# First loads in another order, paired layer 0 runs, and attention's gathers tied to the fourth maximum of a step

## The chip, the core and the metric

The kernel runs on one core of a Trainium2 chip. The core has five engines that work beside each other: TensorE (PE, matmuls and transposes into PSUM), VectorE (DVE), ScalarE (ACT), GpSimd (POOL) and SyncE (SP, which here only starts transfers). The metric is the device time of one execution in microseconds (us), given as the median over several runs.

## What is computed

Four residual layers follow each other on an input of 64 sequences with 64 tokens of 512 features, all in fp32. Each layer is conditional: token arrays pick which weights a sequence uses.

```python
x = x + (einsum('bsi,bio->bso', x, W0[id0]) + b0[id0][:, None])          # layer 0, 16 experts
x = x + (x @ W1 + ((x @ A[id1].T) @ Bm[id1].T) * scalings[id1])          # layer 1, 8 adapters
x = x + attention(x, Wq, Wk, Wv, Wo, k_blocks, v_blocks, tables, kv_lens) # layer 2
x = x + (einsum('bct,bcd->bdt', x, W3[id3]) + side[id3][:, :, None])     # layer 3, 8 subjects

# attention: 8 heads, 4 kv heads, head size 64; q and k are RMS-normed and rotated,
# new k and v are written into a paged cache (blocks of 16) at kv_lens ...,
# each token sees the 256 positions up to its own; softmax over scores * 256 ** -0.5
```

## The kernel before, in words

The 4096 tokens are cut into NT = 32 tiles of 128 tokens, two sequences each. The order of instructions on every engine is the order in which the program is written, since the framework's own scheduler is turned off; waits between engines are semaphores that the framework puts in. An instruction that waits holds up all that is behind it on its engine. SP's transfers also wait for their semaphore lane: eight lanes are used in turn.

**First part.** It makes layers 0 and 1 and the q, k and v of layer 2. `load_x` and `load_w0` bring a tile's input, transposed, and the two 512x512 expert matrices of its two sequences (1 MiB each, `wp` has four buffers, `load_next(i)` asks two tiles ahead). `layer0` multiplies, ACT copies the product to `s0` (L252), POOL adds the bias to x in `add_bias` (L260), PE turns `s0` and DVE adds it in `turn0` (L273, L274): that is x after layer 0, transposed. `layer1` (L612 to L649) takes the tiles in groups, `GROUPS = [1, 1, 2] + [4] * 7`: adapter products `pxa` (L620), masked on DVE into `xa` (L625), the dense products `p1` (L635), and a last product with `xa` (L643), for which PE waits on DVE. `turn_x2` turns a result, `product` makes q or kv (L140), and `turned` (L116 to L135) norms and rotates, on ACT, DVE and POOL. `keep_kv` stores k and v in `kvd`, a copy in DRAM that also gets the old cache rows (`copies`, gathered by POOL and written by SP, L155 and L161). The main loop (L709 to L738) goes over groups: behind layer 1 of group g comes, for each tile of group g + 1, layer 0, `load_next`, `other`, `turn0`, and for each tile of group g `turn_x2`, the q of an earlier tile, and `keep_kv`.

Two things run in pieces beside this on DVE. `rotation(o)` (L365) makes the sines and cosines of eight tiles; `rotation(0)` is made whole behind layer 1 of tile 0. `windows()` (L427) works out the gather indices; `other(i)` takes two of its pieces per tile. `scalars` (L399) prepares the norm gains, `epst`, `eye2` and the first adapter scale.

At the start the token arrays come in by five transfers: `tok1` on SP for register loads, and on ACT's queue `idcol`, `toki` (all tokens in every partition) and later `kvi`, twice; ACT's queue also carries `invf`, `gain` and `tabi`, and half of tile 0's W0, in four chunks.

**Attention.** In step s of the loop at L976, `scores(s)` makes eight score products of 128x320 (L842); DVE adds the mask and finds a maximum for each (L850), ACT takes exponentials with sums (L854). Then PE does `attend(s - 1)` (L889, result copied by DVE at L907), in even steps from 4 on two products of layer 3 (`last`, L929), `project(s - 2)` (L917, added by DVE at L921), `keys(s + 1)` (transposes L823 and L829, copied by ACT to `kT`) and `turn(s)`: 20 transposes of the normalised weights (L875, L879), copied to `pT` by DVE and ACT in turn (L876, L880). DVE normalises at L866, between L907 and L921. All of these but the projection share seven PSUM banks in turn (`ring`), so the third score product waits for the bank of the first pT copy of the step before.

`load_kv(i)` is five gathers on POOL (L769) of 128 rows each, 256 KB, into one of four `kv` buffers. Step s calls it for tile s + 2 at its top; only in steps 0 and 1 a small POOL copy (`after_keys`, L774) holds it until the keys of s are copied. The buffer of tile s + 2 is that of tile s - 2, which `attend(s - 2)` leaves free in step s - 1, so POOL, which has little else, starts the gathers there. Behind them on POOL is `add_one(s - 2)` (L815), which adds the identity to a W3 tile that SP loaded (`load_pair`).

## Time and profile before

| what | value |
|---|---|
| median of 9 runs | 976.68 us (973.21 to 981.08) |
| the profiled execution | 982.19 us, span 980.2 us |
| mean granted TensorE clock | 0.995 |
| PE busy | 933.1 us (95%) |
| DVE, ACT, POOL busy | 608.5, 412.8, 403.3 us |
| DMA | 260.97 MB, 266 GB/s over the span |

In the timeline a row has its start, its length, the engine, the line, the operation, the tile it writes and what it reads, and in brackets how long the engine stood idle before it and what ended that. A row can stand for several like it (x4), its length is then that of all together. In the chain of waits a row is a piece of the chain that ended last. In a table of windows a row has a stretch of time, its length, the busy time and the count of instructions of PE, weight loads, DVE, ACT and POOL, the granted clock, the busy share of DMA and its GB/s.

### The profile page before, as it was taken

To read this page: it belongs to the slowest core of one execution; us is meant where nothing else is said; L and a number is where in the kernel's file an instruction comes from. 1 tells how busy PE (TensorE), PEld (TensorE's weight loads), DVE (VectorE), ACT (ScalarE), POOL (GpSimd) and SP (SyncE) were. 2 spreads that over 40 slices of the span, in tenths; PEclk is the share of its full clock that TensorE was granted. 3 is DMA by queue.
4 is the path that set the end of the run, shared out by engine and by line. 5 is a ranking of instruction groups with operands and counts; after the bars stand their busy time and mean duration, and the time that the engine had idled before them with its cause. 6 is when DMAs were issued, how large, how long until landed. Compare 5 with 4: busy or idle time off the path is not lost.

```text
span 980.2 us, 17784 instructions
## 1 busy us (share of the span) xinstructions
PE 933.1 (95%) x5397; PEld 506.4 (52%) x5397; DVE 608.5 (62%) x1736; ACT 412.8 (42%) x1084; POOL 403.3 (41%) x599
## 2 busy tenths in 40 slices
PE   5999999999999999999999879999999999999998
PEld 1343443444444444444344546766666666666665
DVE  3756898878572363542226858666677666676673
ACT  0212134222341323422223655656666666666663
POOL 3343365554453444444425433444433333344400
PEclk9999999999999999999999989999999999999999
DMA  7988999999999999999954674666565556666521
GB/s 237 348 310 306 371 371 325 387 374 331 391 337 376 391 328 384 364 365 386 342 215 136 219 248 143 210 216 202 179 200 181 186 186 199 195 203 200 185 78 44
DMA packets 133344, 260.97 MB, mean 266 GB/s; under 512 B 32737, under 2 KB 41570, under 8 KB 133250
## 3 DMA queue, kind: packets, MB, share of 16 engines
q1 hardware_dynamic: 108562, 178.61, 50.8%
q0 software_dynamic: 23280, 79.84, 24.5%
q10 hardware_dynamic: 1408, 1.39, 0.5%
q8 instruction: 43, 0.70, 0.3%
q14 instruction: 51, 0.42, 0.1%
HBM read 190.29 MB, written 69.50 MB: 265 GB/s over the span
## 4 chain that ended last, share of the span: by engine, by line
PE 51%; DMA 4%; SPq 2%; DVE 2%; issue 1%; ACT 1%; POOL 0%; ACTq 0%; DVEq 0%; POOLq 0%; another core or an unknown queue 0%
PE py L917 12%; PE po L889 8%; PE ps L842 8%; PE ppt L875 5%; PE pk L140 3%; PE p L635 3%; PE pq L140 2%; PE pkt L823 2%; PE ppt L879 2%; PE p L249 1%; DMA kvd<-st 1%; PE pkt L829 1%; PE pz L929 1%; DMA w<-in_W 1%; DMA st<-in_kvc,cidx 1%
## 5 line engine op out<-in xcount | busy, mean ns | idle before, releaser
L769 POOL DMA_INDIRECT kv<-kvd,idxn x128 | 126.1, 985 | 216.2 <-PE po L889 159.2
L854 ACT ACTIVATE pr<-pr,mx 128x320 f32<-128x320 f32 x256 | 140.1, 550 | 6.3 <-DVE mx L850 3.0
L249 PE MATMUL p<-w,xt 128*64 128x512 f32 x512 | 123.0, 603 | 13.0 <-DMA w<-in_W 12.5
L917 PE MATMUL py<-wo,oT 128*128 128x512 f32 (+1 forms) x264 | 118.3, 592 | 1.7 <-DVE qn L128 1.7
L140 PE MATMUL pk<-wkv,x 128*128 128x512 f32 x256 | 117.1, 602 | 2.7 <-ACT x L656 2.7
L155 POOL DMA_INDIRECT st<-in_kvc,cidx x68 | 67.8, 997 | 113.3 <-DMA kvd<-st 97.3
L635 PE MATMUL p<-w,x 128*128 128x512 f32 x256 | 112.5, 596 | 0.0
L140 PE MATMUL pq<-wq,x 128*128 128x512 f32 x248 | 111.3, 593 | 0.0
L850 DVE CUSTOM_DVE_ANT_0 pr<-ps,mb 128x320 f32<-128x320 f32 x256 | 107.7, 486 | 5.8 <-PE ps L842 2.4
L842 PE MATMUL ps<-kT,qT 64*128 64x320 f32 x512 | 87.4, 460 | 13.4 <-DVE pT L876 8.2
L876 DVE COPY pT<-ppt 128x512 f32<-128x512 f32 x64 | 41.8, 687 | 77.4 <-PE ppt L875 36.0
L866 DVE TENSOR_SCALAR pr<-pr,sm 128x320 f32<-128x320 f32 x256 | 85.4, 395 | 2.3
L889 PE MATMUL po<-pT,kv 128*64 128x128 f32 (+1 forms) x1536 | 84.8, 282 | 1.6 <-issue 1.6
L274 DVE TENSOR_TENSOR x<-pt,x 128x512 f32<-128x512 f32 x32 | 22.0, 688 | 98.2 <-PE pt L273 54.9
L889 PEld LDWEIGHTS po<-pT,kv 128*64 128x64 f32 (+1 forms) x1536 | 70.9, 138 | 22.4 <-DVE mx L850 14.0
L917 PEld LDWEIGHTS py<-wo,oT 128*128 128x128 f32 x264 | 47.5, 189 | 61.6 <-issue 58.4
L249 PEld LDWEIGHTS p<-w,xt 128*64 128x64 f32 x512 | 35.6, 137 | 83.9 <-issue 70.7
L635 PEld LDWEIGHTS p<-w,x 128*128 128x128 f32 x256 | 47.8, 190 | 58.2 <-issue 56.5
L135 POOL TENSOR_TENSOR qr<-qn,sq 128x512 f32<-128x512 f32 x25 | 31.7, 1267 | 106.2 <-DVE qn L134 106.2
L140 PEld LDWEIGHTS pk<-wkv,x 128*128 128x128 f32 x256 | 47.0, 193 | 52.2 <-issue 48.3
L133 DVE TENSOR_TENSOR sq<-qn,sg 128x256 f32<-128x256 f32 (+1 forms) x128 | 40.1, 355 | 49.7 <-POOL sg L110 47.7
L140 PEld LDWEIGHTS pq<-wq,x 128*128 128x128 f32 x248 | 44.9, 190 | 46.2 <-issue 46.2
(191 smaller groups left out, 1322.9 us busy)
## 6 DMA issues: line engine op xcount, KB each, us to landing
w<-in_W SPq DMA_DIRECT2D x62, 1024.0 KB
kvd<-st SPq DMA_DIRECT2D x68, 512.0 KB
xt<-in_xT SPq DMA_DIRECT2D x32, 256.0 KB
x2d<-x2n SPq DMA_DIRECT2D x32, 256.0 KB
kvd<-kvn SPq DMA_DIRECT2D x32, 256.0 KB
qTd<-qTs SPq DMA_DIRECT2D x32, 256.0 KB
qT<-qTd SPq DMA_DIRECT2D x32, 256.0 KB
x2r<-x2d SPq DMA_DIRECT2D x32, 256.0 KB
```

What stands on the lines that cost most here:

```text
L140: TE.matmul(ps, x2s[i][:, c, :], w[:, c, :], start=c == 0, stop=c == KC - 1)
L155: P.indirect_dma_start(out=st, out_offset=None, in_=a["kvc"].rearrange("(n r) d -> n (r d)", r=2), in_offset=bass.IndirectOffsetOnAxis(ap= ...
L249: TE.matmul(p0[hs, :], xs[i][:, c, hs], w0s[i][h][:, c, :], start=c == 0, stop=c == KC - 1)
L635: TE.matmul(p1[i], x1s[i][:, c, :], w1[:, c, :], start=c == 0, stop=False)
L769: P.indirect_dma_start(out=kv[:, n, :], out_offset=None, in_=kvd, in_offset=bass.IndirectOffsetOnAxis(ap=at, axis=0),)
L842: TE.matmul(ps[g2][:, :NPOS], qT[rows, gp, b2].rearrange("p h t -> p (h t)"), kT[rows, gp, b2 * NPOS : (b2 + 1) * NPOS], start=True, stop= ...
L850: V.tensor_tensor_reduce(out=p, in0=ps[g2][:, :NPOS], in1=mb[:, b2, :], scale=-1.0, scalar=3.0e38, op0=ALU.add, op1=ALU.min, accum_out=mx[ ...
L854: S.activation(p, p, AF.Exp, bias=mx[:, g, b2 : b2 + 1], scale=-1.0, accum_out=sm[:, g, b2 : b2 + 1],)
L866: V.tensor_scalar(p, p, sm[:, g, b2 : b2 + 1], None, ALU.mult)
L875: TE.transpose(pt[:, n * 128 : (n + 1) * 128], pr[:, g, at : at + 128], ident)
L889: TE.matmul(po[b2][g2 * 64 : (g2 + 1) * 64, gp * 128 : (gp + 1) * 128], kv[rows, n, (G + g) * HD : (G + g + 1) * HD], pT[rows, c, m * 128 ...
L917: TE.matmul(py[:, fs], oT[:, c].rearrange("p b t -> p (b t)"), wo[:, c, fs], start=c == 0, stop=c == KC - 1,)
```

## The change

**The start.** `idcol`, `toki` and `kvi` are no longer loaded: DVE makes `tok1` a row of floats and PE spreads it by small matmuls into a PSUM bank, from which they are read or cast. `invf`, `gain` and `tabi` go to SP, behind `wkv`. The chunks of tile 0's W0 are issued in turn on SP and ACT with both row numbers read first. The bias is turned ahead of the last chunk's products, and `turn0(0)` is done in two halves. `scalars` keeps the gains alone and moves, with `rotation(0)`, behind `turn0(1)`.

**Layer 0 in pairs.** Where the next group is twice as large, the first tile of a pair keeps its `s0` (two buffers now) and is turned behind the second one's layer 0. `other` takes none of the windows' pieces at tile 1 and four at tile 2.

**Attention.** `keys(0)` moves ahead of the last q product of the passage. In every step the gathers of tile s + 2 come behind `scores(s)`, and a POOL copy of the fourth maximum of that step stands in front of them.

```diff
         nc.sync.dma_start(tok1.rearrange("p k b -> p (k b)"), a["toks"])
-        idcol = su.tile([B, 1], I32, name="idcol")
-        nc.scalar.dma_start(idcol, a["toks"][:, 0:B].rearrange("o b -> b o"))
-        toki = su.tile([128, 4, B], I32, name="toki")
-        nc.scalar.dma_start(toki.rearrange("p k b -> p (k b)"), a["toks"].partition_broadcast(128))
-        invf = su.tile([128, HALF], F32, name="invf")
-        nc.scalar.dma_start(invf, a["invf"].partition_broadcast(128))
-        nc.scalar.dma_start(
-            gain.rearrange("p k h f -> p (k h f)"), a["gains"].partition_broadcast(128)
-        )
         make_identity(nc, ident)
...
         P.iota(pidx, pattern=[[0, 1]], base=0, channel_multiplier=1)
+        one = su.tile([1, 128], F32, name="one")
+        V.memset(one, 1.0)
+        tokf = su.tile([1, 4, B], F32, name="tokf")
+        V.tensor_copy(tokf, tok1)
+        ptok = bank("ptok")
+        TE.matmul(ptok[:B, 4 * B : 4 * B + 1], tokf[:, 0, :], one[:, :1], start=True, stop=True)
+        for h in range(2):
+            TE.matmul(
+                ptok[h * B : (h + 1) * B, 4 * B + 1 : 4 * B + 2], tokf[:, 3, :], one[:, :1], start=True, stop=True
+            )
+        TE.matmul(ptok[:, : 4 * B], one, tokf.rearrange("p k b -> p (k b)"), start=True, stop=True)
+        toki = ptok[:, : 4 * B].rearrange("p (k b) -> p k b", k=4)
+        idcol = su.tile([B, 1], I32, name="idcol")
+        V.tensor_copy(idcol, ptok[:B, 4 * B : 4 * B + 1])
+        kvi = su.tile([128, 1], I32, name="kvi")
+        V.tensor_copy(kvi, ptok[:, 4 * B + 1 : 4 * B + 2])
         brow = su.tile([B, D], F32, name="brow", tag="valp")
...
-            w0s[i] = []
-            for b, queue in zip((2 * i, 2 * i + 1), queues):
-                w = wp.tile([128, KC, D], F32, name="w")
-                r = queue.value_load(tok1[0:1, 0, b : b + 1], min_val=0, max_val=E - 1)
-                for n in range(parts):
-                    cs = slice(n * KC // parts, (n + 1) * KC // parts)
-                    queue.dma_start(
-                        w[:, cs], a["W0"][bass.ds(r, 1)].rearrange("a (c p) o -> p (a c) o", p=128)[:, cs]
+            w0s[i] = [wp.tile([128, KC, D], F32, name="w") for _ in range(2)]
+            def row(h):
+                b = 2 * i + h
+                return queues[h].value_load(tok1[0:1, 0, b : b + 1], min_val=0, max_val=E - 1)
+            first = [row(h) for h in range(2)] if parts > 1 else []
+            for n in range(parts):
+                cs = slice(n * KC // parts, (n + 1) * KC // parts)
+                for h in range(2):
+                    r = first[h] if first else row(h)
+                    queues[h].dma_start(
+                        w0s[i][h][:, cs],
+                        a["W0"][bass.ds(r, 1)].rearrange("a (c p) o -> p (a c) o", p=128)[:, cs],
                     )
-                w0s[i].append(w)
...
             for c in range(KC):
+                if c == KC - 1 and not bias:
+                    turn_bias()
                 for h in range(2):
...
             w0s.pop(i)
-            s0 = s0s[i] = wk.tile([128, D], F32, name="s0")
+            s0 = s0s[i] = wk.tile([128, D], F32, name="s0", bufs=2)
             S.copy(s0, p0)
...
-        def turn0(i):
+        def turn0(i, parts=1):
...
             pt = bank("pt")
-            for c in range(KC):
-                TE.transpose(pt[:, c * 128 : (c + 1) * 128], s0[:, c * 128 : (c + 1) * 128], ident)
-            V.tensor_tensor(x1, pt.rearrange("p (c t) -> p c t", c=KC), x1, ALU.add)
+            for n in range(parts):
+                lo, hi = n * KC // parts, (n + 1) * KC // parts
+                for c in range(lo, hi):
+                    TE.transpose(pt[:, c * 128 : (c + 1) * 128], s0[:, c * 128 : (c + 1) * 128], ident)
+                V.tensor_tensor(
+                    x1[:, lo:hi], pt[:, lo * 128 : hi * 128].rearrange("p (c t) -> p c t", t=128), x1[:, lo:hi], ALU.add
+                )
...
         load_weight(wkv, "wkvT")
-        kvi = su.tile([128, 1], I32, name="kvi")
+        invf = su.tile([128, HALF], F32, name="invf")
+        nc.sync.dma_start(invf, a["invf"].partition_broadcast(128))
+        nc.sync.dma_start(gain.rearrange("p k h f -> p (k h f)"), a["gains"].partition_broadcast(128))
         tabi = su.tile([128, NBLK], I32, name="tabi")
         for h in range(2):
-            hs = slice(h * B, (h + 1) * B)
-            nc.scalar.dma_start(kvi[hs], a["toks"][:, 3 * B :].rearrange("o b -> b o"))
-            nc.scalar.dma_start(tabi[hs], a["tab"])
+            nc.sync.dma_start(tabi[h * B : (h + 1) * B], a["tab"])
...
         adf = su.tile([128, 8, 8], F32, name="adf")
-        V.tensor_copy(adf.rearrange("p o q -> p (o q)"), toki[:, 1, :])
-        V.tensor_tensor(adf, adf, bc(mine[:, None, :], [128, 8, 8]), ALU.mult)
+        V.tensor_tensor(
+            adf, toki[:, 1, :].rearrange("p (o q) -> p o q", q=8), bc(mine[:, None, :], [128, 8, 8]), ALU.mult
+        )
         ado = su.tile([128, 8], F32, name="ado")
...
             V.tensor_copy(gsw[:, :, 1, :], gain[:, :, 0, :])
-            V.memset(epst, EPS)
-            V.tensor_tensor(eye2, ident[:, :64], ident[:, 64:], ALU.add)
-            scale_b(0)
+        V.memset(epst, EPS)
+        V.tensor_tensor(eye2, ident[:, :64], ident[:, 64:], ALU.add)
+        scale_b(0)
...
         bg, old, turns, asked, made = windows(), copies(kvd[:OLD], op, 3), {}, [], []
+        held = []
...
-        scalars()
         biasT = su.tile([128, KC, B], F32, name="biasT")
+        def turn_bias():
+            pb = bank("pb")
+            for c in range(KC):
+                TE.transpose(pb[:, c * B : (c + 1) * B], brow[:, c * 128 : (c + 1) * 128], ident[:B, :B])
+            S.copy(biasT.rearrange("p c b -> p (c b)"), pb[:, : KC * B])
         layer0(0, False)
-        pb = bank("pb")
-        for c in range(KC):
-            TE.transpose(pb[:, c * B : (c + 1) * B], brow[:, c * 128 : (c + 1) * 128], ident[:B, :B])
-        S.copy(biasT.rearrange("p c b -> p (c b)"), pb[:, : KC * B])
         add_bias(0)
-        turn0(0)
+        turn0(0, 2)
         load_next(0)
...
-            next(bg, None)
-            next(bg, None)
+            for _ in range(0 if i == 1 else 4 if i == 2 else 2):
+                next(bg, None)
...
             layer1(tiles[g])
-            if g == 0:
-                run(rotation(0))
-            elif g == 1:
+            if g == 1:
                 far()
...
                     load_b(i0 // 4 + 1)
-                if i is not None:
-                    turn_x2(i)
-                q = asked.pop() if asked and i is not None else None
+                if i is None:
+                    held.append(i0)
+                    continue
+                turn_x2(i)
+                if held:
+                    turn0(held.pop())
+                q = asked.pop() if asked else None
                 if q is not None:
...
                 turn0(i0)
+                if g == 0:
+                    scalars()
+                    run(rotation(0))
                 if q is not None:
...
                     made.append(q)
-                if i is not None:
-                    keep_kv(i, product(i, wkv, "pk"), P)
-                    if i < NT - LATE:
-                        asked.append(i)
-                    if len(made) > 1:
-                        turn_q(made.pop(0))
+                keep_kv(i, product(i, wkv, "pk"), P)
+                if i < NT - LATE:
+                    asked.append(i)
+                if len(made) > 1:
+                    turn_q(made.pop(0))
         layer1(tiles[-1])
...
-    kvs, kTs, mbs, prs, pTs, oTs, qTs, pairs, x3s = {}, {}, {}, {}, {}, {}, {}, {}, {}
+    kvs, kTs, mbs, prs, mxs, pTs, oTs, qTs, pairs, x3s = {}, {}, {}, {}, {}, {}, {}, {}, {}, {}
...
-    def after_keys(i):
+    def after_scores(i):
         seen = bp.tile([1, 1], F32, name="seen")
-        P.tensor_copy(seen, kTs[i][0:1, 0, 0:1])
+        P.tensor_copy(seen, mxs[i][0][0:1, 1, 1:2])
...
         pr = bp.tile([128, G, 2 * NPOS], F32, name="pr")
-        mx = bp.tile([128, G, 2], F32, name="mx")
+        mxs[i] = [bp.tile([128, 2, 2], F32, name=f"mx{gp}") for gp in range(2)]
         sm = bp.tile([128, G, 2], F32, name="sm")
...
                         out=p, in0=ps[g2][:, :NPOS], in1=mb[:, b2, :], scale=-1.0, scalar=3.0e38,
-                        op0=ALU.add, op1=ALU.min, accum_out=mx[:, g, b2 : b2 + 1],
+                        op0=ALU.add, op1=ALU.min, accum_out=mxs[i][gp][:, g2, b2 : b2 + 1],
                     )
                     S.activation(
-                        p, p, AF.Exp, bias=mx[:, g, b2 : b2 + 1], scale=-1.0, accum_out=sm[:, g, b2 : b2 + 1],
+                        p, p, AF.Exp, bias=mxs[i][gp][:, g2, b2 : b2 + 1], scale=-1.0, accum_out=sm[:, g, b2 : b2 + 1],
                     )
...
     for i in range(NT - LATE + 1, NT - 1):
+        if i == NT - 2:
+            keys(0)
         pq = product(i, wq, "pq")
...
         next(parts[i])
-    keys(0)
     load_q(1)
...
         if s + 2 < NT:
-            if s < 2:
-                after_keys(s)
-            load_kv(s + 2)
             load_mask(s + 2)
...
         scores(s)
+        if s + 2 < NT:
+            after_scores(s)
+            load_kv(s + 2)
         if s >= 2:
...
         if s:
```

## The prediction

> **What bounds the kernel now.** I read the page first, then the chain of waits, the timeline of the first 60 us, of 540 to 610 us and of two late attention steps, and last the windows around 580 us. The page says that TensorE is the bound nearly everywhere:
>
> ```profile
> span 980.2 us, 17784 instructions
> PE 933.1 (95%) x5397; PEld 506.4 (52%) x5397; DVE 608.5 (62%) x1736; ACT 412.8 (42%) x1084; POOL 403.3 (41%) x599
> PEclk9999999999999999999999989999999999999999
> ```
>
> So only 47 us are without a matmul, and a gain must come out of these, or out of time in which PE is counted as busy but slow. They lie in three places. The first is the start: layer 0 of tile 0 ends at 16.6 us, and later PE waits for the next weights.
>
> ```profile
> 3.90 4.44 ACTq L232 DMA_DIRECT2D w<-in_W  x4
> 18.70 1.57 SPq L232 DMA_DIRECT2D w<-in_W  x2
> 19.82 1.09 PE L620 MATMUL pxa<-x,ao 128*32 128x128 f32 x8 [1.90 <-DVE x L274]
> 28.03 3.65 PE L249 MATMUL p<-w,xt 128*64 128x512 f32 x14 [1.44 <-DMA w<-in_W]
> ```
>
> The second is the passage into attention: a 2.9 us stall, then 6.8 us at half clock (0.50 in the third row).
>
> ```profile
> 576.77 2.01 PE L842 MATMUL ps<-kT,qT 64*128 64x320 f32 x10 [2.92 <-ACT pT L876]
> 575.00:580.00 5.00, 2.63 (x11) 1.52 (x12) 2.46 (x7) 3.82 (x7) 0.25 (x1) 0.84 0.73 234
> 580.00:585.00 5.00, 5.00 (x46) 3.93 (x48) 2.20 (x12) 4.99 (x16) 0.00 (x0) 0.50 0.24 65
> ```
>
> The third is every attention step. Here is the same spot twice, in a step with gathers and in one of the last steps, which have none:
>
> ```profile
> 849.73 1.91 PE L875 MATMUL ppt<-ident,pr 128*128 128x128 f32 x16
> 849.80 0.95 POOL L769 DMA_INDIRECT kv<-kvd,idxh  x1 [0.30 <-issue]
> 851.92 1.29 DVE L876 COPY pT<-ppt 128x512 f32<-128x512 f32 x2 [2.39 <-PE ppt L875]
> ...
> 951.19 1.91 PE L875 MATMUL ppt<-ident,pr 128*128 128x128 f32 x16
> 951.83 0.69 DVE L876 COPY pT<-ppt 128x512 f32<-128x512 f32 x1 [0.84 <-PE ppt L875]
> ```
>
> Without gathers the first pT copy starts 0.64 us behind the first transpose; with them 2.19 us, and ACT's starts beside it (852.04). In nearly all the steps with gathers it starts 1.1 to 1.3 us after the fifth gather's issue ends (850.75 here). The trace's semaphore events say how: PE's signals come on time until about 4.5 us after the first gather, then stop but for a stray one, and from 7.2 us on drain 0.06 us apart. The chain shows what the late copies cost, since scores need their banks:
>
> ```profile
> 915.23 0.74 PE ps L842 x4
> 916.00 0.70 DVE pT L876
> 916.74 1.95 PE ps L842 x12
> ...
> 928.95 2.58 PE ps L842 x16
> ...
> 940.93 2.35 PE ps L842 x16
> ...
> 953.54 2.35 PE ps L842 x16
> ```
>
> From scores to scores, an even step (with L929's two products, 0.86 us) takes 13.72 us with gathers and 12.61 without; an odd one 11.98, and 12.61 - 0.86 = 11.75 without.
>
> **The start, cost by cost.** Out go six DMAs of token data and constants in front of ACT's half of W0, and lane waits behind them (SP's third and fourth chunk are issued at 5.68 and 7.81, as toki and gain land). In come three small DVE operations (0.15 to 0.2 us each) and a handful of tiny matmuls (0.3 us each at most); all of it, under 2 us, fits between the tokens' landing at 3.4 and the first W0 landing at 8.7, so it costs nothing; without that cover, 2 us. SP gains four issues (invf, gain, twice tabi, 0.4 to 0.6 each, 2 us) behind wkv; queued behind them are tile 2's loads, landed at 41.3 for a use at 42.3, with SP some 6 us earlier: nothing.
>
> DMA moved 356 GB/s at 10 to 15 us, 210 at 15 to 20. With x and W0 of tile 0 (2.36 MB) first, from 3.5 us, they are in by 10.1, with landing 11.3, against 15.5. The bias is turned ahead of the last chunk's matmuls, its 1.47 us on POOL leave the path, and turn0 in halves gives up 0.3 more: pxa at 15.5 instead of 19.82. The bias gather can eat 1 us of this (it took 7.8 us to land). W0 of tile 1 (2.1 MB, behind w1 and the gathers) lands near 21.6, so layer 0 of tile 1 ends at 25.3 instead of 31.6.
>
> But DVE takes it back. rotation(0), 21.37 to 28.93 = 7.6 us, and scalars, 1.1, used to run beside layer 1 of tile 0; now they stand behind turn0(1), at 27.1. Then the kv chain (ACT square to xa, 36.68 to 40.78 = 4.1, plus 0.4 for the cosine): xa at 40.3, before 40.8. PE has only pk, pxa and p1 to do and waits some 5 us. Two window steps (28.85 to 33.86, 5.0) move to tile 2, where DVE runs without a gap: mask to 44.0, four steps 10.2, two more 5.5, two turn0 1.4, so x1 of tile 3 at 61.1 and pxa at 61.2, before 59.36: 1.8 late. The pairs take away ACT's copy of s0 from PE's path: 0.77 each at 46.7 (inside that wait), 72.9 and 90.8, so 1.5 won. Sum: 0.3 lost. Bounds: 4 won, if DVE gets its gain rows earlier and PE keeps its lead; 3 lost, if POOL slows DVE. I take 0.3 lost, as the DVE rows add up to it.
>
> **The passage.** keys(0) goes ahead of the last q product: its 1.1 us and the 0.98 wait leave PE's path, but DVE starts the first maxima at 552.77 either way; 0.8 is left. The gathers for tile 2 move from 551.6 to 555.1, so their quiet end (7.2 later, 562.3) now delays step 0's pT by 2.5: scores(1) end at 565.0, 1.2 late. Those for tile 3 start at 566 (before 560.4), tile 4's at 577 (before 568.8), out of the stretch in which DMA was 0.92 to 1.05 busy. Then scores(2) run to 576 instead of 580.8, po at full clock, py waits 1.8 for DVE's qn as before (1.69), and scores(3) start at 587.3, before 594.1: 6.8 won. Of this 3.4 is half clock. Bounds: 1 lost (the new quiet end stalls a short step, with the half clock staying) to 9 won.
>
> **The steps.** POOL's copy (0.18) waits for the fourth maximum. Queued behind it are five gathers and add_one. Maxima come every 0.41 us from 0.45 after scores start, so gathers start at 2.6 to 2.9 of the step; before, at 5 (odd) or 4.8 (even) of the step ahead: 10 us later in all. Who waits: keys, whose rows land by 10.5 and are read about 20 us into this count, so 9 us spare; add_one, needed a step later, 12 us spare. PE's quiet stretch then is 7.5 to 10.0. In it end py and the key transposes; ACT's key copies go from 9.1 to 10.0 and end at 11.5, DVE's x3 goes from 8.6 to 10.0 and pT from 10.2 to 10.7 to 11.4. The third score matmul, which needs that bank, comes at 12.1. So a step nears that without gathers: from scores(3) at 594.08 to scores(30) at 940.93 there are 13 even and 14 odd steps, 13 x 12.61 + 14 x 11.75 + 0.9 for two q turns = 329.3 against 346.85: 17.5 won. ACT's later copies have 0.2 to 0.5 us of slack; I take 16. Bounds: 0 (quiet stretch costs elsewhere) to 17.5.
>
> A rule speaks against this term. The Trainium skill, SBUF — State Buffer, section "Who interferes with whom", says that DMA never contends with a compute engine and that PE and ACT wait on no one; by it the gathers' place would not matter and this term would be 0, the sum 975.7. The late signals of 27 steps say otherwise, and I go by them.
>
> Sum against the profiled execution (980.2 span, 982.19 in all): + 0.3 - 6.8 - 16 = 959.7. That run is 5.5 over the median of 976.68; I hold its half clock (3.4) for part of that surplus, as it is the one disturbance the trace shows. This the change has already taken out, so 2.1 are left to take off: 958.
>
> **Rivals.** *The quiet stretch catches po.* If it starts less than 2.3 us after the first gather, DVE's oT copy waits to 10.0, normalising (3.1) ends near 13.8, the last transposes near 15.2: 2.4 us over today's 12.85, 27 times, 65 us: about 1035, slower. For it: in the saturated step at 560 signals already lagged 3.0 after the first gather. Against: all steps from 599 on show signals on time past 4.2. 6%. *The steps stay as they are*, the quiet stretch costing as much under py as under the transposes, or not coming from the gathers: 958 + 16 = 974. For it: in the step at 560 PE itself stood still 1.6 us in po. Against: there 48 short matmuls ran into it, here eight long ones. 9%. *Half of it*: ACT, with res before the key copies in even steps, becomes late: 966. 13%. *The start carries through*, 4 won: 954. 12%. The forecast: 60%.
>
> **How the numbers follow.** 958 is the likeliest case. The forecast's own range is 950 to 965; with the carried start and the half gain 947 to 970, which leaves the 974 and 1035 cases and tails outside. A measurement of this kernel tells 0.3% (2.9 us) from no change, so faster means under 973.8. The forecast, the carried start and the half gain are all faster (85%), and of the 974 case 4 in 9: 0.89. The other 5% are the same, the po case 0.06 slower.
>
> **What would show it.** Right: gathers 2.6 to 2.9 us behind the start of scores; the first pT copy about 1 us behind its transpose; mean step 12.2 to 12.3; scores(3) near 587; no 0.50 window there. pxa of tile 0 near 15.5, xa of tile 1 near 40, pxa of tiles 2 and 3 near 61. Wrong: pT copies still 2 us late, or DVE waiting at L907 for po; a first L643 of tile 1 before 37 would mean that the start carries.

## The result, and the profile after

The changed kernel takes 1046.3 us (median of 10 runs, 1041.18 to 1054.01), against 976.25 us before (31 runs): a ratio of 1.072, 95% interval 1.070 to 1.074. The forecast was 958 us, faster; it is 70 us slower. The profiled execution took 1044.65 us with a span of 1042.9 us. Three lines of the page after:

```profile
span 1042.9 us, 17846 instructions
PE 964.5 (92%) x5405; PEld 524.5 (50%) x5405; DVE 605.1 (58%) x1740; ACT 412.5 (40%) x1084; POOL 404.6 (39%) x627
PEclk9899998999999999999999799999999999999999
```

PE has the same matmuls (eight tiny ones more), but is busy 31.4 us longer and idle 31 us longer: half of the loss is waiting; the other half is time in which PE counts as busy but gets on slowly. By place, from the first score product of a step to that of another:

| stretch | before | after | difference | forecast |
|---|---|---|---|---|
| start to scores(0) | 550.87 | 550.47 | -0.4 | +0.3 |
| scores(0) to scores(3) | 43.14 | 51.39 | +8.3 | -6.8 |
| scores(3) to scores(30) | 346.85 | 401.64 | +54.8 | -16 |

The first row flatters the change: the execution before that it is held against is late there, and another trace of the same kernel (before, again, below) reaches scores(0) at 544.33.

**A step.** In the kernel before, po ends at 844.31 in a late step, 0.3 us ahead of the first gather, and DVE copies it at once. The key transposes then run under the gathers, and ACT copies their first result on time too, 4.6 us behind the first gather:

```profile
844.35 0.76 DVE L907 COPY oT<-po 128x256 f32<-128x256 f32 x2 [0.65 <-PE po L889]
844.64 0.96 POOL L769 DMA_INDIRECT kv<-kvd,idxn  x1 [6.32 <-PE po L889]
848.64 0.82 PE L823 MATMUL pkt<-ident,kv 128*128 128x128 f32 x6
849.22 0.86 ACT L824 COPY kT<-pkt 128x384 f32<-128x384 f32 x2 [2.69 <-PE pkt L823]
```

These are five rows of the timeline of the changed kernel in an odd step, whose scores start at 868.84:

```profile
871.20 2.56 PE L917 MATMUL po<-pT,kv 128*64 128x128 f32 x48
872.37 0.99 POOL L797 DMA_INDIRECT kv<-kvd,idxn  x1 [0.54 <-issue]
877.41 0.95 POOL L797 DMA_INDIRECT kv<-kvd,idxh  x1 [0.30 <-issue]
880.01 0.76 DVE L935 COPY oT<-po 128x256 f32<-128x256 f32 x2 [6.86 <-remote]
881.34 1.33 PE L903 MATMUL ppt<-ident,pr 128*128 128x128 f32 x8 [2.85 <-DVE pr L894]
```

The gathers are issued from 872.37 to 878.36. po ends at 873.76, 1.4 us behind the first of them, and PE goes on to py and the keys. But DVE's copy of oT, which waits for nothing but po, starts at 880.01: 6.2 us late and 1.65 us behind the end of the last issue. The profile cannot name what released it ("remote"). Normalising stands behind that copy on DVE, the transposes of the weights behind normalising, and PE waits 2.85 us. In the semaphore events no signal of PE comes between 871.32 and 879.99; then eight come within 0.4 us.

**The clock.** Half clock follows the waits. One stretch of the table of windows, behind the first long wait in the start (0.52 is the granted clock):

```profile
40.00:45.00 5.00, 4.21 (x8) 1.26 (x10) 3.05 (x10) 0.59 (x1) 4.28 (x7) 0.52 0.50 151
```

Between scores(3) and scores(30) the granted clock falls to 0.50 nine times for 3.4 us, in nine of the twelve places where PE had waited 2.1 to 2.9 us (in one of the nine in two pieces, of 0.99 and 1.12). All nine drops start on one grid of 3.413 us (from 613.66 to 702.41 are 26 such lengths); why the other three waits have none behind them is open. Of the 54.8 us, 29.9 are more idle time of PE (39.8 instead of 10.0). The rest is a longer busy time, up to 15.4 of it (9 x 3.4 x 0.5) by half clock. Nearly all of this rest, 24.1 us, lies in the transposes of the weights right behind the late normalising (PE is busy in them for 87.69 us instead of 63.58); po takes 69.25 us in both kernels.

**The passage** shows the same, harder, in step 1. The gathers for tile 3 start at 567.77, 0.4 us behind the start of po:

```profile
567.77 0.97 POOL L797 DMA_INDIRECT kv<-kvd,idxn  x1 [0.16 <-issue]
...
575.22 0.76 DVE L935 COPY oT<-po 128x256 f32<-128x256 f32 x2 [6.21 <-PE pkt L851]
576.53 3.41 PE L903 MATMUL ppt<-ident,pr 128*128 128x128 f32 x16 [0.53 <-DVE pr L894]
```

po ends at 569.91, so oT is 5.3 us late. Between the two rows PE itself steps through the key transposes one by one (one of 0.27 us at 572.16 stands behind 1.09 us without a matmul), and the transposes at 576.53 run at half clock (3.41 us for what takes 1.91). In step 2, po's late signals also keep DVE from qn, for which py waits 7.3 us (1.69 before), and then runs at half clock:

```profile
593.36 5.29 PE L945 MATMUL py<-wo,oT 128*128 128x512 f32 x8 [7.33 <-DVE qn L128]
```

Step 0, which has no po, loses as well: from its scores to those of step 1 are 14.32 us, before 10.53. There DVE's maxima start at 554.51 (552.77 before), the q product runs at half clock, and the pT copies come late under the gathers for tile 2.

**The start** went as forecast in its rows, up to the clock:

```profile
40.46 0.28 DVE L646 TENSOR_TENSOR xa<-pxa,own 32x128 f32<-32x128 f32 x1
40.80 2.07 PE L664 MATMUL p<-bo,xa 32*128 32x512 f32 x2 [5.21 <-DVE xa L646]
```

xa of tile 1 was forecast at 40.3 and came at 40.46, pxa of tiles 2 and 3 at 61.2 and came at 60.65. The 0.52 in the window at 40 us was not forecast.

### The profile page after: what moved, and what is told of

Read it like the earlier page. It is cut to its first block, busy times and chain, and to the rows that moved or that the text cites. A ratio compares the mean times of both kernels' runs of the same rounds, so it can differ in the third digit from the quotient of the medians.

```text
span 1042.9 us, 17846 instructions
## 1 busy us (share of the span) xinstructions
PE 964.5 (92%) x5405; PEld 524.5 (50%) x5405; DVE 605.1 (58%) x1740; ACT 412.5 (40%) x1084; POOL 404.6 (39%) x627
## 4 chain that ended last, share of the span: by engine, by line
PE 58%; DVE 10%; another core or an unknown queue 5%; issue 2%; DMA 1%; ACT 1%; POOL 0%; SPq 0%; DVEq 0%; ACTq 0%
PE py L945 8%; PE p L656 7%; PE pk L140 6%; PE pq L140 6%; PE ppt L903 6%; PE ps L870 5%; PE po L917 5%; PE p L264 5%; DVE pr L894 3%; DVE pr L878 3%; PE pkt L857 2%; DVE oT L935 2%; PE pkt L851 2%; PE ppt L907 1%
## 5 line engine op out<-in xcount | busy, mean ns | idle before, releaser
L797 POOL DMA_INDIRECT kv<-kvd,idxn x128 | 123.0, 961 | 52.8 <-issue 46.1
L935 DVE COPY oT<-po 128x256 f32<-128x256 f32 x64 | 25.5, 422 | 164.2 <-remote 67.6
L903 PE MATMUL ppt<-ident,pr 128*128 128x128 f32 x512 | 84.4, 311 | 37.7 <-DVE pr L894 36.0
L805 POOL COPY seen<-mx 1x1 f32<-1x1 f32 x30 | 5.3, 177 | 241.0 <-DVE mx L878 229.1
L903 PEld LDWEIGHTS ppt<-ident,pr 128*128 128x128 f32 x512 | 62.6, 157 | 57.7 <-DVE pr L894 35.5
L870 PE MATMUL ps<-kT,qT 64*128 64x320 f32 x512 | 84.3, 455 | 1.7 <-DVE qn L128 1.4
L894 DVE TENSOR_SCALAR pr<-pr,sm 128x320 f32<-128x320 f32 x256 | 83.2, 389 | 2.3
L917 PE MATMUL po<-pT,kv 128*64 128x128 f32 (+1 forms) x1536 | 82.1, 278 | 0.0
L291 DVE TENSOR_TENSOR x<-pt,x 128x512 f32<-128x512 f32 (+1 forms) x33 | 22.0, 672 | 98.1 <-PE pt L290 86.6
```

Of the source, the lines that this page charges most:

```text
L797: P.indirect_dma_start(out=kv[:, n, :], out_offset=None, in_=kvd, in_offset=bass.IndirectOffsetOnAxis(ap=at, axis=0),)
L870: TE.matmul(ps[g2][:, :NPOS], qT[rows, gp, b2].rearrange("p h t -> p (h t)"), kT[rows, gp, b2 * NPOS : (b2 + 1) * NPOS], start=True, stop= ...
L894: V.tensor_scalar(p, p, sm[:, g, b2 : b2 + 1], None, ALU.mult)
L903: TE.transpose(pt[:, n * 128 : (n + 1) * 128], pr[:, g, at : at + 128], ident)
L917: TE.matmul(po[b2][g2 * 64 : (g2 + 1) * 64, gp * 128 : (gp + 1) * 128], kv[rows, n, (G + g) * HD : (G + g + 1) * HD], pT[rows, c, m * 128 ...
```

## The experiments

The theory after the result: PE's signals of po, due while POOL issues gathers, are held until the issue is over, and everything in a step hangs on po's. Rivals: the bytes that arrive do it, not the issue; the rows come too late; the start or the passage has a share. The mean step below is the time from scores(3) to scores(30) over 27; ratios are to runs of before on the same chip, with their 95% intervals.

| kernel | median us | ratio | mean step |
|---|---|---|---|
| before, again | 975.35 | 0.999 (0.998 to 1.001) | 12.82 |
| changed | 1046.3 | 1.072 (1.070 to 1.074) | 14.88 |
| gathers back | 980.07 | 1.009 (1.008 to 1.011) | 12.72 |
| gathers alone | 1026.85 | 1.055 (1.053 to 1.057) | 14.53 |
| plain loads | 958.57 | 0.982 (0.979 to 0.984) | 12.20 |
| short rows | 1045.42 | 1.071 (1.067 to 1.074) | 14.86 |
| first maximum | 1072.93 | 1.105 (1.103 to 1.107) | 15.68 |
| behind oT | 1008.02 | 1.040 (1.037 to 1.043) | 13.71 |
| project first | 1063.99 | one run | 15.45 |
| no 64 rows | 974.87 | 1.001 (0.999 to 1.003) | 12.57 |
| 64 rows first | 1029.55 | 1.058 (1.053 to 1.062) | 14.20 |
| four gathers | 962.25 | 0.989 (0.985 to 0.993) | 12.21 |
| split gathers | 956.98 | 0.983 (0.981 to 0.984) | 12.20 |
| split and start | 955.74 | 0.981 (0.980 to 0.983) | 12.20 |
| rotation early | 987.65 | 1.012 (1.010 to 1.015) | 12.84 |
| start fixed | 977.93 | 1.006 (1.004 to 1.008) | 12.74 |
| start even | 974.11 | 1.001 (0.999 to 1.003) | 12.69 |

### Which part of the change it is

**Gathers back.** The changed kernel with the gathers where they were.

```diff
         if s + 2 < NT:
+            if s < 2:
+                after_keys(s)
+            load_kv(s + 2)
             load_mask(s + 2)
...
         scores(s)
-        if s + 2 < NT:
-            after_scores(s)
-            load_kv(s + 2)
```

> The changed kernel with one part undone: the gathers stand again at the top of a step and start as soon as po has released the buffer; start, pairs and keys(0) stay as changed. Theory (the loss is the gathers' place alone: PE's signals of po are held under them): scores(3) to scores(30) takes 347 us again, scores(0) starts near 550.5 as in the changed kernel, and keys(0) ahead of the q product gives 0.8, so 975 to 976 us, within 0.3% of before. Rival (start, pairs and keys(0) have a share of the loss, by the 5.2 us wait and the half clock behind it): over 980 us.

Measured: 980.07 us, 1.009. The steps are back at 12.72 us, so the gathers' place makes the loss there; but 0.9%, 8.8 us by the ratio, stays with the start, the pairs and keys(0), against 0.3 lost and 0.8 won in the forecast. The theory's 975 to 976 us failed; the rival's share of the start is there.

**Before, again**, without an edit:

> The kernel before, unchanged, for a trace on the same chip as the other runs. Every theory: within 0.3% of the runs of before beside it; steps from scores(3) to scores(30) about 345 us. Its start and its passage are what those of the gathers-back kernel are to be held against.

Measured: 975.35 us, 0.999. Its scores(0) start at 544.33, against 550.87 in the execution that the prediction was summed against, and it has the same 6.8 us at half clock in the passage. So what that execution had above the median lay ahead of attention, not in the half clock.

**Gathers alone.** The kernel before with load_kv and the copy of the fourth maximum behind scores, and nothing else of the change.

```diff
         if s + 2 < NT:
-            if s < 2:
-                after_keys(s)
-            load_kv(s + 2)
...
         scores(s)
+        if s + 2 < NT:
+            after_scores(s)
+            load_kv(s + 2)
```

> The kernel before with the gathers behind the fourth maximum of a step and nothing else of the change. Theory: the whole loss but the start's share of some 8 us: 1.06 to 1.065 of before. Rival (the loss needs the changed passage or keys(0) as well): under 1.05.

Measured: 1026.85 us, 1.055, 53.5 us. That is most of the loss, but under what was expected. The two parts alone make 53.5 + 8.8 = 62.3 us; together they make 70. Part of the rest is in the steps (392.3 us from scores(3) to scores(30) here, 401.6 in the changed kernel): with the gathers at the same 3.52 us, the second oT copy of an even step comes at 7.8 us here and at 9.3 there. Why is open.

### The issue or the bytes

**Plain loads.** POOL only writes one element of each part; SP loads the bytes. The gather by index is left out.

```diff
+    def plain_kv(i, j):
+        kv = kvs[i] = kvp.tile([128, 5, 2 * G * HD], F32, name="kv")
+        P.tensor_copy(kv[0:1, :, 0], mxs[j][0][0:1, 1:2, 1].to_broadcast([1, 5]))
+        for n in range(5):
+            at = (5 * i + n) * 128 % NTOK
+            nc.sync.dma_start(kv[:, n, :], kvd[at : at + 128, :])
...
-            after_scores(s)
-            load_kv(s + 2)
+            plain_kv(s + 2, s)
```

> The changed kernel, but from step 0 on POOL writes one element of each kv part behind the fourth maximum and SP then loads the same 5 x 256 KB into it as plain rows (the gather by index is left out, other rows come). The bytes arrive at the same time as in the changed kernel; POOL issues no gathers. Theory I (POOL's issue of the gathers holds PE up): oT is copied on time, 4.95 to 5.3 us into each step, steps 11.8 and 12.6 in turn, about 970 us or less. Theory II (the arriving bytes hold PE up): oT late as in the changed kernel, near 1046 us.

Measured: 958.57 us, 0.982. A step of its timeline, and the window from scores(3) to scores(30), in which PE's busy time is the whole stretch:

```profile
860.28 0.76 DVE L942 COPY oT<-po 128x256 f32<-128x256 f32 x2 [0.64 <-PE po L924]
...
586.40:915.82 329.42, 329.42 (x2867) 230.98 (x2867) 243.86 (x843) 218.03 (x625) 12.77 (x55) 1.00 0.66 205
```

The same bytes behind the same maximum cost nothing: oT is copied as po ends, PE has no idle time in 27 steps, and the steps take 11.75 and 12.61 us. This is the floor that the prediction had worked out from the last steps (329.3 us).

**Short rows.** As many gathers, at the same maximum, an eighth of the bytes, into a tile that nobody reads; the cache beyond four tiles is left out.

```diff
+        if i > 3:
+            kvs[i] = first[i % 4]
+            short = bp.tile([128, 5, 64], F32, name="short")
+            for n in range(5):
...
+                    out=short[:, n, :], out_offset=None, in_=kvd.rearrange("r (n c) -> (r n) c", c=64),
```

> The changed kernel, but from tile 4 on each step's five gathers fetch rows of 256 bytes, an eighth, into a tile that nobody reads, and attention goes on with the kv of the first four tiles (so the rest of the cache is left out). As many gathers are issued as in the changed kernel, at the same maximum, with an eighth of the bytes. Theory I (POOL's issue): oT 7.3 us behind the first gather in odd steps as in the changed kernel, near 1040 us. Theory II (the bytes): oT on time or under 1 us late, 975 us or less.

Measured: 1045.42 us, as slow as the changed kernel, with the same picture. po ends at 906.03, the first gather is issued at 904.66, and the last one and oT are:

```profile
909.71 0.94 POOL L801 DMA_INDIRECT short<-kvd,idxh  x1 [0.30 <-issue]
912.04 0.75 DVE L947 COPY oT<-po 128x256 f32<-128x256 f32 x2 [6.61 <-PE pkt L869]
```

The two runs settle that the bytes do not do it, and that gathers issued on POOL do. The landing of the rows does not set the end of the hold either: in the step of the kernel before that is shown above, the held signals come from 851.90 on, and packets of the same gathers go on until 853.97. Whether POOL's own work in an issue or what its transfer queue does beside it holds the signals, no run separates.

### What sets how late they are

**First maximum.** The copy reads `mxs[i][0][0:1, 0, 0:1]`.

> The changed kernel, but the POOL copy waits for the first maximum of a step, not the fourth: gathers start three maxima (3 x 0.41 = 1.23 us) earlier. Theory 1 (PE's signals are held until about 1.2 us after the last gather has been issued): the signals of po come 1.2 us earlier in each of 27 steps, so at least 33 us less, about 1010 us, and less still where half clock falls away. Theory 2 (a signal of po is late by a fixed time, some 6 us, once it has met the gathers): no change, 1046 us.

Measured: 1072.93 us, slower, where one theory had 1010 and the other no change. In odd steps oT does come 1.25 us earlier in the step (9.6 instead of 10.9), with the end of the issue; in even steps, where po's two signals had got through early in the changed kernel (at 7.9 and 9.3), it comes at 9.4. But now po runs under the whole issue, and PE itself stops in its last products, which use 64 rows. Two of these stops, 0.7 us from product to product, and the oT copy behind them:

```profile
879.65 0.31 PE L917 MATMUL po<-pT,kv 64*64 64x128 f32 x1 [0.43 <-issue]
880.35 0.27 PE L917 MATMUL po<-pT,kv 64*64 64x128 f32 x1 [0.39 <-issue]
882.75 0.76 DVE L935 COPY oT<-po 128x256 f32<-128x256 f32 x2 [5.26 <-PE po L917]
```

The first gather was issued at 875.36, the last one's issue ended at 881.36. po ends 5 to 9 us into odd steps instead of 4.9, and py behind it.

**Behind oT.** The copy reads what attend(s - 1) made in this step.

```diff
             attend(s - 1)
+            if s + 2 < NT:
+                seen = bp.tile([1, 1], F32, name="seen")
+                P.tensor_copy(seen, oTs[s - 1][0:1, 0, 1, 0:1])
+                load_kv(s + 2)
```

> The changed kernel, but from step 1 on the POOL copy reads the oT that attend(s - 1) makes in this step: the gathers of tile s + 2 start only when po's signals have come, at 5.4 to 6.5 of the step, though they are as late in the program as in the changed kernel. Theory (what counts is that no po is under the gathers): steps as in before, 12.8 us in the mean, 973 to 980 us. Rival (the loss comes from gathers a step later, whose rows land late for keys, or from the extra POOL copy): near 1046 us.

Measured: 1008.02 us: oT is on time, but the steps take 13.71 us, which neither side had. The copy waits for the second oT copy, so the first gather comes 1.7 us behind the end of po (875.11), not 0.3, and the issue runs into the next step's scores, which start at 880.24:

```profile
880.28 0.95 POOL L797 DMA_INDIRECT kv<-kvd,idxh  x1 [0.30 <-issue]
881.77 0.59 ACT L904 COPY pT<-ppt 128x512 f32<-128x512 f32 x1 [2.97 <-PE ps L870]
```

The later pT copies wait for the end of the last issue (881.23). So it is not that rows come late; what counts is which signals fall under the issue.

**Project first.** py ahead of po in a step.

```diff
+        if s > 2:
+            project(s - 2)
         if s:
             load_pair(s - 1)
             attend(s - 1)
...
-        if s >= 2:
+        if s == 2:
             project(s - 2)
```

> The changed kernel with project(s - 2) ahead of attend(s - 1) from step 3 on, so that eight long matmuls (py) run under the first gathers and the 48 short ones of po under the last. Theory A (every signal due between the first gather and 1.2 us behind the last is held): DVE's addition to x3 waits to about 7.5 us behind the first gather although py ends 2.6 us behind it. Theory B (the short matmuls of po bring the hold about): the addition starts on time, right behind py, and only oT is late. Time in both cases near that of the changed kernel, 1030 to 1060 us, since po's signals come no earlier.

Measured: 1063.99 us, with Theory B's picture:

```profile
885.06 0.99 POOL L797 DMA_INDIRECT kv<-kvd,idxn  x1 [0.54 <-issue]
887.63 0.69 DVE L949 TENSOR_TENSOR x<-py,x2r 128x512 f32<-128x512 f32 x1 [1.78 <-issue]
890.79 0.38 PE L917 MATMUL po<-pT,kv 64*64 64x128 f32 x2 [0.72 <-issue]
892.50 0.76 DVE L935 COPY oT<-po 128x256 f32<-128x256 f32 x2 [4.17 <-PE po L917]
```

py runs from 883.89 to 887.59; its signal, of eight long products, is on time 2.5 us behind the first gather. The short products of po stop, and their signal comes 1.4 us behind the end of the last issue (891.07).

**No 64 rows** and **64 rows first.** In attend, the second loop (16 products with 64 rows) is left out, with the shared part of the cache; or it goes ahead of the first loop.

```diff
-                        product(b2, g, slice(0, 128), n, g, n, gp == 0 and c == 0, False)
-        for gp in range(2):
-            for b2 in range(2):
-                for g in (2 * gp, 2 * gp + 1):
-                    product(b2, g, slice(b2 * 64, (b2 + 1) * 64), 4, G, g, False, gp == 1)
+                        product(b2, g, slice(0, 128), n, g, n, gp == 0 and c == 0, gp == 1 and c == 1)
```

> The changed kernel without the 16 products of 64 rows at the end of attend (the part of the cache shared by a pair is left out of the sum); the 32 of 128 rows stay, under the gathers' issue as before. Theory S (the 64-row products, which run on a quarter of the array, are what POOL's issue holds up): oT on time, 13 us less work than before in all steps and no late signals, 970 us or less. Theory N (any short matmuls): oT still over 3 us late in odd steps, 1010 us or more.

> The changed kernel with the 16 products of 64 rows ahead of the 32 of 128 rows in attend, so that they run from 2.4 to 3.1 us of a step and are over when the first gather is issued at 3.5. Theory S: oT on time, near 980 us (the start's share of the loss stays). Theory N: as in the changed kernel, near 1046 us.

Measured: 974.87 and 1029.55 us. Theory S falls, since oT is late in both; Theory N's times (1010 or more, and 1046) are missed too. With the 64-row products first, po's first half is copied 0.7 us behind the first gather, on time; the second half is due at 866.35 and comes at 872.27, 1.3 us behind the end of the last issue (870.96):

```profile
864.95 0.99 POOL L797 DMA_INDIRECT kv<-kvd,idxn  x1 [0.54 <-issue]
865.66 0.42 DVE L935 COPY oT<-po 128x256 f32<-128x256 f32 x1
872.27 0.42 DVE L935 COPY oT<-po 128x256 f32<-128x256 f32 x1 [6.19 <-PE pkt L857]
```

Without them the second oT copy is still late in odd steps, by 1.9 to 5.7 us, but the first one is on time and the second is let go earlier, often before the issue is over. That kernel gains 2.3 us a step, of which 0.6 is po's shorter time; so the 64-row products, or their number, have a part in how long the hold is. The stop inside PE is not theirs alone either: in the kernel before, it comes twice among po's 128-row products in the saturated step at 560 us.

```profile
566.01 0.38 PE L889 MATMUL po<-pT,kv 128*64 128x128 f32 x2 [0.50 <-issue]
567.47 1.01 PE L889 MATMUL po<-pT,kv 128*64 128x128 f32 x18 [1.09 <-issue]
```

**Four gathers.** Gathers back, with the fifth one as a plain load on SP (its index left out).

```diff
+            if n == 4 and i > 3:
+                nc.sync.dma_start(kv[:, n, :], kvd[i * 128 : i * 128 + 128, :])
+                continue
```

> The gathers-back kernel, but from tile 4 on the fifth gather is a plain load on SP (the index of that part is left out, other rows come), so POOL issues four. Theory I (PE's signals are held until about 1.2 us behind the last issue): pT copies 1.25 us earlier in each step, even steps 12.7 instead of 13.7, about 14 us less than gathers back, 0.995 of before. Rival (the quiet time is fixed by the first gather, 4.5 to 7.2 us behind it): no change, 1.009 of before.

Measured: 962.25 us, 0.989: 18 us less than gathers back (2.0% of before, by the ratios), and steps of 11.75 and 12.61.

```profile
871.97 0.95 POOL L800 DMA_INDIRECT kv<-kvd,idxn  x1 [0.30 <-issue]
873.80 1.29 DVE L907 COPY pT<-ppt 128x512 f32<-128x512 f32 x2 [1.70 <-PE ppt L906]
```

The first pT copy still comes 0.9 us behind the end of the last issue (872.92), but that is now 1.5 us behind the start of the transposes (872.29), and the scores' bank is free in time. The hold ends 5.7 us behind the first gather (868.07) instead of 7.2, so it follows the last issue and is no fixed time. The 17 us that the kernel before loses per execution come from one gather too many in a row.

### What the start loses

**Rotation early.** Gathers back, with scalars and rotation(0) behind layer 1 of tile 0.

```diff
             layer1(tiles[g])
+            if g == 0:
+                scalars()
+                run(rotation(0))
```

> The gathers-back kernel with rotation(0) and scalars once more behind layer 1 of tile 0, where the kernel before has rotation(0); DVE is idle there from 18.2 to 27.4 us in the changed kernel. Theory (the 0.9% that the gathers-back kernel loses come from the wait of 5.2 us for xa of tile 1 and the 6.8 us at half clock behind it, 3.4 lost): xa of tile 1 near 35 us, no wait over 1 us there, some 8 us less than gathers back, about 972 us. Rival (the loss lies in the pairs, in keys(0) or in the loads on SP): at most 3 us less.

Measured: 987.65 us, worse than gathers back. The gains land at 26.5 us, DVE waits 7.7 us for them, and ACT's sines now stand in front of the s0 copy of tile 1, which comes at 35.16 and for which PE waits 9.1 us:

```profile
26.52 0.23 DVE L421 TENSOR_SCALAR gain<-gain 128x128 f32<-128x128 f32 x1 [7.69 <-DMA gain<-in_gains]
35.78 1.12 PE L290 MATMUL pt<-ident,s 128*128 128x128 f32 x4 [9.12 <-ACT s L267]
```

So this run does not test the theory: the loads that the change moved to SP come too late for an earlier rotation.

**Start fixed** and **start even.** invf and gain go out on ACT's queue behind its half of W0, the rotation stands behind layer 0 of tile 1; then also the windows' pieces are two and two again.

```diff
         load_w0(0, KC, (nc.sync, nc.scalar))
+        nc.scalar.dma_start(invf, a["invf"].partition_broadcast(128))
+        nc.scalar.dma_start(gain.rearrange("p k h f -> p (k h f)"), a["gains"].partition_broadcast(128))
...
                 layer0(i0)
+                if g == 0:
+                    scalars()
+                    run(rotation(0))
...
-            for _ in range(0 if i == 1 else 4 if i == 2 else 2):
+            for _ in range(2):
```

> The gathers-back kernel with invf and gain issued on ACT's queue right behind its half of tile 0's W0 (in the rotation-early kernel the gains landed at 26.5 us and ACT's sines stood in front of the s0 copy of tile 1), and scalars with rotation(0) behind layer 0 of tile 1. Theory (what the changed start loses is the wait for xa of tile 1 and the half clock behind it): no wait over 1.5 us between 27 and 40 us, xa of tile 1 near 35 us, 8 us less than gathers back, 0.99 to 1.00 of before. Rival (the small loads slow tile 0's W0, or DVE ends rotation late again): no better than gathers back, 1.01 of before.

> The start_fixed kernel with the windows' pieces two and two again (none at tile 1 and four at tile 2 in the changed kernel). Theory (the four pieces make pxa of tiles 2 and 3 wait for DVE, and the half clock follows from the wait): no wait over 1.5 us at 55 to 62 us, 5 to 6 us less than start_fixed, 0.995 to 1.00 of before. Rival (the pairs or keys(0) lose it): 1.004 or more.

Measured: 977.93 us, 1.006, and 974.11 us, 1.001. Start fixed misses its 0.99 to 1.00. In it the longest wait between 27 and 40 us is 1.85 us, and the next one is at tiles 2 and 3, where DVE's four pieces of the windows stand ahead of x; in start even it is gone:

```profile
58.56 2.52 PE L641 MATMUL pxa<-x,ao 128*32 128x128 f32 x16 [3.01 <-DVE x L291]
```

```profile
58.43 1.10 PE L641 MATMUL pxa<-x,ao 128*32 128x128 f32 x16
```

So, by the ratios, each known to some 2 us, 3.2 us of the start's 8.8 went with the rotation's place and 4.7 with the pieces; what is left of the start, the pairs and keys(0) is worth nothing that can be measured (0.1%, interval -0.1 to +0.3).

### A version that beats both

**Split gathers.** The kernel before; four gathers stay behind po, the fifth is issued in the next step behind its first maximum.

```diff
-            load_kv(s + 2)
+            load_kv(s + 2, range(4))
...
         scores(s)
+        if s + 2 < NT:
+            seen = bp.tile([1, 1], F32, name="seen")
+            P.tensor_copy(seen, mx0[s][0:1, 0, 0:1])
+            load_kv(s + 2, range(4, 5))
```

> The kernel before, with the gathers of a tile split: four behind po as now, the fifth in the next step behind its first maximum, 2.2 us into the step. Theory I (PE's signals due under an issue are held until about 1.2 us behind the last of it): the lone gather's hold is over at 4.4, po's signals are due at 4.9, and four behind po cost nothing, so steps of 11.75 and 12.61, 14 to 17 us less, 0.983 to 0.987 of before. Rival (any gather under the short products of po holds its signals up, or stops PE in them): oT late in each step, 1.00 of before or more.

> The gathers split as in split_gathers, with the changed start of start_even. Theory: the gains add up, 14 to 17 us from the split and 3 or 4 from the start and the pairs: 0.98 of before. Rival (the start's small gain goes where DVE and DMA are full): 0.985 to 0.99.

Measured: 956.98 us, 0.983 (0.981 to 0.984), and with the start of start even 955.74 us, 0.981 (0.980 to 0.983): the two do not differ by more than their intervals, so the start adds nothing that is shown. A step of split gathers, and its window from scores(3) to scores(30):

```profile
848.14 0.98 POOL L769 DMA_INDIRECT kv<-kvd,idxh  x1 [0.16 <-DMA w<-in_w3b]
851.25 0.76 DVE L909 COPY oT<-po 128x256 f32<-128x256 f32 x2 [0.64 <-PE po L891]
857.30 0.69 DVE L878 COPY pT<-ppt 128x512 f32<-128x512 f32 x1 [0.87 <-PE ppt L877]
...
589.99:919.40 329.41, 329.41 (x2867) 230.94 (x2866) 245.46 (x843) 217.33 (x625) 143.56 (x187) 1.00 0.64 199
```

The lone gather is issued from 848.14 to 849.12, under the start of po (848.65 to 851.21); po's signals are due 2 us later and come on time. The four follow from 851.55 to 856.41, and the first pT copy is on time too. Five gathers a step cost nothing when no more than four follow each other and none of PE's urgent signals is due before they are through.

## Why the prediction was wrong, point by point

**The steps: the step that failed.** The prediction read in the kernel before that signals come on time until about 4.5 us behind the first gather and then stop until 7.2, and moved that picture to 2.6 to 2.9 us of the step as if it were a fixed time. But what it had seen in these 4.5 us was another load of PE: mainly py, eight long products whose signal is due at the end, then the first key transposes. It called what would run under the gathers "eight long ones"; in fact 27 of po's 48 short products do, and po, due at 4.92 us of the step, ends 1.4 us behind the first gather, which comes at 3.52 (the copy starts at 2.81; its 0.18 and the 0.54 behind it on POOL were left out). Project first shows the difference directly: under the same gathers py's signal is on time and po's is not. What the runs show in its place is that po's signals, due 1.4 us behind the first gather, are held, and in nearly all odd steps let go only 1.2 to 1.7 us behind the end of the last issue, 10.8 to 11.2 us into the step; with plain loads they come at 4.95. Term: 16 won, measured 54.8 lost.

**The rival that came true** was the first, that the quiet stretch catches po, at 1035 us and 6%. Its mechanism and its size a step (2.4 us forecast; 401.64 - 346.85 over 27 gives 2.03, half clock included) were right, and its condition was met (a quiet stretch that starts under 2.3 us behind the first gather: po, due 1.4 us behind it, is held). What was wrong is its 6%: the evidence for it, the saturated step at 560 us where po met the gathers, was set aside with a wrong description of the step to come. That the total of 1046 lies near its 1035 is in part chance: the steps lost less than its 65 us, and the passage 15 us more than was forecast.

**The size of what could be won was right.** The prediction's floor of 329.3 us for 27 steps is what plain loads and split gathers take (329.4). Only the way there was wrong: not later gathers, but fewer in a row.

**The passage**: 6.8 won, measured 8.3 lost, in steps 1 and 2 by the same mistake; in step 0 (3.8 of the 8.3) by half clock, later maxima and late pT copies. The wait of py for qn, put at 1.8 us, took 7.3. The gathers for tile 3 start at 567.77 as forecast (566), and po under them delays oT. scores(2), forecast to be over at 576, start at 580.31, and scores(3) at 601.86 instead of 587.3.

**The start**: 0.3 lost was the forecast, and the rows added up (xa of tile 1 and pxa of tiles 2 and 3 within 0.6 us of the forecast; pxa of tile 0 at 16.57 instead of 15.5). What was left out is that a wait of PE is followed by half clock: 6.8 us at 0.50 from 40.2 us, 3.4 lost. Gathers back puts the whole at 8.8 us; the two edits to the start name 7.9 of them.

**The anchor**: the half clock was taken for the surplus of the profiled execution; the trace of before, again, has it too and is 6.5 us shorter ahead of scores(0).

**The rule that spoke against the change**, the Trainium skill, SBUF — State Buffer, section "Who interferes with whom" (DMA never contends with a compute engine, PE waits on no one), is borne out for the bytes: plain loads move them while po and py run, for nothing. It gave 0 for the step's term, and for gathers that POOL issues that is wrong by 54.8 us; the measurement decides. No run shows that the hold lies in SBUF, of whose ports the page speaks.

## What to carry to other kernels

Before gathers are moved on POOL, list the signals of PE that fall due from the first issue to two microseconds behind the end of the last, and ask who waits for each; put a row of gathers under long products that signal once, and split it when it is longer than these. A quiet stretch seen in one place says nothing of another where PE runs other instructions: read which signals were due in it, not only which came. And price a wait of PE of 2 us or more with the half clock that may follow it.

## What the runs showed of the hardware that was not expected

- PE's signals are late while POOL issues indirect gathers: up to 6 us for a row of five (6.0 us of issue), whatever the bytes (rows of 2 KB, 1.072 of before, or of 256 bytes, 1.071). ACT's signals come on time in the same stretch where the changed kernel has any: those of two exponentials, at 874.31 and 874.85, while po's of 873.76 waits until 879.99.
- Which signals are held is open. That of eight 128x512 products was on time 2.5 us behind the first gather (project first), that of po was not 1.4 us behind it, and the short key transposes of the kernel before signalled on time 4.6 us behind it; so neither the time nor the length of a product decides alone. The number of products that PE has begun since the first gather fits these cases: at most 14 for the signals on time (py 5, the first half of po in 64 rows first 8, those key transposes 14), 23 or more for the late ones (its second half 23, po in the changed kernel 27). No run tests it, and even steps speak for more than that: they let two of po's signals through early (typically at 7.9 and 9.3 us of the step, odd steps at 10.9).
- Later in a row PE itself stops between its products, for 0.4 to 1.1 us each in the rows shown here, at po's products of 64 and of 128 rows and at key transposes. What inside the chip does either is open.
- The granted clock fell to 0.50 for 3.4 us behind nine of twelve waits of 2.1 to 2.9 us. The Trainium skill, TensorE: Matmul & The Clock Gate, section "Part 1: The HAM clock gate (the "warmup" mystery)", asks for an idle window of about 3.4 us; here no wait in the steps was that long, so shorter ones are enough. In the 3.41 us ahead of these nine drops PE was busy for 0.9 to 1.8 us.
